# A three-pass attention and convolution kernel: first loads into buffers that are free early, strips and taps of the first image in turn, and a sum of k kept in another PSUM bank

## The chip, the cores and the metric

The kernel runs on one core of a Trainium2 chip (trn2). The metric is the device time of one execution in microseconds (us). Everything is float32. Engines are named as in the profile: PE is the tensor engine (PEld its weight loads), DVE the vector engine, ACT the scalar engine, POOL the GpSimd engine, SP the engine whose queue issues every DMA of this kernel. Each engine works through its own instructions in a fixed order and waits on semaphores for the others.

## What is computed

Eight images of 256 channels and 64 x 64 pixels go through two layers.

```
# layer 0: attention against keys and values of a 16 x 16 reduced image
xr  = layernorm_over_channels(conv4x4_stride4(x, w_sr)) * g + b
q   = w_q x ;  k, v = split(w_kv xr)               # 8 heads of 32
x   = x + gamma * w_out (softmax(q k^T / sqrt(32)) v)

# layer 1: linear attention on two scales
qkv = w_qkv x                                       # 3 * 256 channels
agg = w_pw (depthwise5x5(qkv))                      # 8 x 8 per group
for both (qkv, agg), in heads of 8 channels:
    kv  = sum over pixels of relu(k) (v, 1)^T       # 8 x 9; the last column is the sum of k
    att = (relu(q) kv)[:8] / ((relu(q) kv)[8] + 1e-15)
out = x + batchnorm(w_proj concat(att))
```

## The kernel before, in words

The work is three functions, called one after the other, with results handed on through DRAM. All loops are unrolled in Python. The code gives each tile a pool, a tag and a number of buffers; a tile framework then places pools in SBUF, one behind the other in the order in which a pass opens them, and derives every semaphore. A pass's pools lie over those of the pass before it, so a tile's first write waits until whatever tile lay there has been used for the last time. The framework also sets the order on each engine: an instruction that is ready in its own estimate may be put ahead of one that stands earlier in the code but isn't ready. In the trace, for example, the stores of zeros `border` (L624, called once an image) all stand on SP in the first stretch, and the copy L1129 stands some 7 us ahead of L1130, which follows it in the code.

**First pass** (`first_pass`, L575). `load_x(0)` issues the eight strips of image 0 (L599, 512 KB each), then seven constants are loaded (L589). `keys_values(0)` (L653) goes through 16 taps of the 4 x 4 convolution: each loads a weight tile `wsr` (256 KB, L662, four buffers) and does matmuls at L665. Tap f reads columns 256 f to 256 f + 255 of the image, so strip s (512 columns) holds what taps 2s and 2s + 1 read. Mean, variance, scale, k and v follow (L679 to L728). Then a loop over image, strip, channel half and key half does scores (L752), exponentials (L758), values (L769), denominators (L785), output (L803) and, six steps behind, qkv (L828). The next image's `keys_values` and the second pass's convolution weights (`conv_weights`, L632) are fed in between. Images alternate between two buffers of 32 KB a partition. qkv goes to DRAM as `planes`, keys as `kd`, values as `vd`.

**Second pass** (`second_pass`, L946). 64 units (two channel halves t, four groups k, eight images b; b innermost). A unit loads a convolution weight `w` (1.5 MB, once per eight units and kind, L963), cells `d` (578 KB, L969, one for keys and values and one for queries), tokens `kq` (512 KB, L976) and `vq` (four DMAs of 384 KB, L986). DVE makes differences of neighbouring cells, `c` (L996, L997, in `paired`); PE convolves them (L1054 and L1058, three banks `cv`). In `summed_raw` PE forms kv of the unconvolved keys (L1079) in a single bank, `raw`. In `summed` it does the same for the convolved ones (L1096). The sums of k are matmuls with a vector of ones. The bank `few` holds three results of a unit in turn: the k sum of the raw part, in column 0 (L1127, `ended_raw`), the k sum of the convolved part, in column 128 (L1135, `ended`), and the spread kv (L1142, `spread`). `ended_raw` copies kv out of `raw` (L1129) and the k sum out of `few` (L1130) into `mraw`, which is stored (L1131). `applied` (L1166) forms numerator and denominator in the bank pair `ng`, DVE divides (L1169, L1171) and transposes (L1178), and the result `att` is stored (L1180). The loop over u works on four units at once: the raw sum and first convolution of u, the sums of u - 1, the query convolution of u - 2, `applied` of u - 3. In the code, `summed_raw(u)` stands at the head of step u, and `ended_raw(u - 1)` in its middle.

**Third pass** (`third_pass`, L1230). 64 steps (image, half, class). `load_sums` (L1245) reads the kv sums of an image in eight DMAs (L1250) and spreads them over a mask; `loads` reads `raw` (L1275), `xs` (L1284) and `agg` (L1295). `flat` makes relu(q) (L1308), `applied` (L1343) the numerator, PE turns it (L1361), and `proj` (L1379) projects; ACT scales (L1388), DVE adds (L1397), and the result is stored (L1404). The code calls `loads(0)` ahead of its constants, and `loads(n + 2)` at each step n.

Of the kernel before, what the change touches and what calls it, by code (L numbers as in the profile page):

```python
# [574 lines left out]
def first_pass(ctx: ExitStack, tc: tile.TileContext, a, fine, planes, x2d, kd, vd, wtd):  # L575
# [4 lines left out]
    xpool = ctx.enter_context(tc.tile_pool(name="xpool", bufs=2))  # L580
# [6 lines left out]
    def load(src, name):  # L587
        t = const.tile(list(src.shape), F32, tag=name, name=name)
        nc.sync.dma_start(t, src)  # L589
        return t  # L590

    x_tiles = {}

    def load_x(b):
        x_tiles[b] = xpool.tile([P, 2, HW], F32, tag="x", name=f"x_{b}")
        src = a.xp[b].rearrange("(c p) n -> p c n", p=P)
        for s in range(NG):
            cols = slice(s * QB, (s + 1) * QB)
            nc.sync.dma_start(x_tiles[b][:, :, cols], src[:, :, cols])  # L599

    load_x(0)
    vec = load(a.vecs, "vec")
    wkv = load(a.w_kv, "wkv")
    wq = load(a.w_q, "wq")
    gam = load(a.gamma_s, "gam")
    wout = load(a.w_out, "wout")
    wqkv = load(a.w_qkv, "wqkv")
    wsmall = load(a.w_small, "wsmall")
# [11 lines left out]
    nil = const.tile([NB2 + 2, 8 * P], F32, tag="nil", name="nil")  # L620
# [11 lines left out]
    def conv_weights():  # L632
        for j in (2, 3, 0, 1):
# [4 lines left out]
            for i in range(8):  # L638
# [5 lines left out]
                    wsmall[:, j, gs].unsqueeze(2).to_broadcast([P, 2, 6 * 16, D1]),  # L644
# [8 lines left out]
    def keys_values(b):  # L653
# [51 lines left out]
        for ci in range(2):  # L705
            nc.vector.tensor_mul(xr[:, ci], xr[:, ci], rs)
            nc.vector.tensor_scalar(
                xr[:, ci], xr[:, ci], vec[:, 0, ci : ci + 1], vec[:, 1, ci : ci + 1], ALU.mult, ALU.add
            )
# [4 lines left out]
        for oc in range(2):  # L714
            ps = bank(f"k_{b}_{oc}")[:, :NK]
            for ci in range(2):
                nc.tensor.matmul(
                    ps, wkv[:, ci, oc * P : (oc + 1) * P], xr[:, ci], start=(ci == 0), stop=(ci == 1)
                )
            nc.scalar.copy(kk[:, oc], ps)  # L720
        yield
        for kc in range(2):
            ps = bank(f"v_{b}_{kc}")[:, :C]
            for ci in range(2):
                nc.tensor.matmul(
                    ps, xr[:, ci, kc * P : (kc + 1) * P], wkv[:, ci, C:], start=(ci == 0), stop=(ci == 1)
# [7 lines left out]
    def queries(b, s, c):  # L734
        ps = bank(f"q_{b}_{s}_{c}")
        for ci in range(2):
            nc.tensor.matmul(  # L737
                ps,
                wq[:, ci, c * P : (c + 1) * P],
# [59 lines left out]
    def added(b, s, att, oc):  # L799
        xt, cols = x_tiles[b], slice(s * QB, (s + 1) * QB)  # L800
        ps = bank(f"o_{b}_{s}_{oc}")
        for c in range(2):
            nc.tensor.matmul(ps, wout[:, c, oc * P : (oc + 1) * P], att[c], start=(c == 0), stop=(c == 1))  # L803
        nc.vector.scalar_tensor_tensor(  # L804
            xt[:, oc, cols], ps, gam[:, 0:1], xt[:, oc, cols], ALU.mult, ALU.add
# [19 lines left out]
    def qkv(b, s, st, j):  # L825
        ps = bank(f"qkv_{b}_{s}_{j}")
        for ci in range(2):
            nc.tensor.matmul(  # L828
                ps,
                wqkv[:, ci, j * P : (j + 1) * P],  # L830
# [35 lines left out]
    for _ in keys_values(0):  # L866
# [3 lines left out]
    q, es, att, fill = {0: queries(0, 0, 0)}, {}, {}, []  # L870
# [75 lines left out]
def second_pass(ctx: ExitStack, tc: tile.TileContext, a, planes, kd, vd, wtd, kvd, attd):  # L946
    nc = tc.nc
    B = a.x.shape[0]
    const = ctx.enter_context(tc.tile_pool(name="const2", bufs=1))
    two = ctx.enter_context(tc.tile_pool(name="two2", bufs=2))  # L950
# [7 lines left out]
    wt, data, cells, kqs, vqs = {}, {}, {}, {}, {}  # L958

    def load_weights(u, what):  # L960
        t, k, b = units[u]
        w = two.tile([P, 4, 6 * P], F32, tag=f"w{what}", name=f"w{what}_{t}_{k}")
# [3 lines left out]
    def load_cells(u, what):  # L966
        t, k, b = units[u]
        d = two.tile([P, 4, (NB + 1) ** 2], F32, tag=f"d{what}", name=f"d{what}_{u}", bufs=2)
        nc.sync.dma_start(d, planes[b, 2 * what + t][4 * k : 4 * k + 4].rearrange("g p e -> p g e"))  # L969
        data[u, what] = d.rearrange("p g (y x) -> p g y x", x=NB + 1)  # L970


    def load_tokens(u):
        t, k, b = units[u]
        kq = two.tile([P, 2, 4, P], F32, tag="kq", name=f"kq_{u}")
# [5 lines left out]
        vq = two.tile([P, 4, 6 * P], F32, tag="vq", name=f"vq_{u}", bufs=3)  # L981
# [9 lines left out]
    def paired(u, what):  # L991
        d = data[u, what]
        c = two.tile([P, 2 + what, 4, (NB + 1) * NB // 2], F32, tag=f"c{what}", name=f"c{what}_{u}")
# [28 lines left out]
    eps = const.tile([P, 1], F32, tag="eps", name="eps")  # L1022
# [19 lines left out]
    def convolve(u, what, i):  # L1042
        t, k, b = units[u]
        c, w, d = cells[u, what], wt[t, k, what], data[u, what]
# [77 lines left out]

    def ended_raw(u):
        t, k, b = units[u]
        few[u] = bank("few", f"few_{u}")
        col, ps = few[u][:, :1], raws.pop(u)
# [4 lines left out]
        nc.sync.dma_start(kvd[b, t][k], m)  # L1131

    def ended(u):
        col, m = few[u][:, 128:129], state[u, "m"]
# [5 lines left out]
    def spread(u):  # L1140
        ps = few.pop(u)[:, 256 : 256 + D0 + 4]
# [88 lines left out]
def third_pass(ctx: ExitStack, tc: tile.TileContext, a, planes, x2d, kvd, attd, out):  # L1230
    nc = tc.nc
    B = a.x.shape[0]
    const = ctx.enter_context(tc.tile_pool(name="const3", bufs=1))
    two = ctx.enter_context(tc.tile_pool(name="two3", bufs=2))
# [10 lines left out]
    def load_sums(b):  # L1245

        kvp = two.tile([P, 2, 4, D0 + 1], F32, tag="kvp", name=f"kvp_{b}")
        for t in range(2):
            for k in range(4):
                nc.sync.dma_start(  # L1250
                    kvp[k * D0 : (k + 1) * D0, t], kvd[b, t][k].rearrange("(f d) n -> d f n", f=4)
                )
        nc.vector.tensor_add(kvp[:, :, :2], kvp[:, :, :2], kvp[:, :, 2:])
        kva = two.tile([P, 2, D0 + 1], F32, tag="kva", name=f"kva_{b}")
        nc.vector.tensor_add(kva, kvp[:, :, 0], kvp[:, :, 1])

        m = two.tile([P, 2, P + NH], F32, tag="kvm", name=f"kvm_{b}")
# [10 lines left out]
    def loads(n):  # L1268
# [3 lines left out]
        raw = two.tile([P, 2, 4, 8 * (NB + 1)], F32, tag="raw", name=f"raw_{n}", bufs=3)  # L1272
# [9 lines left out]
        xs = two.tile([P, 2, 4, P], F32, tag="xs", name=f"xs_{n}", bufs=4)  # L1282
# [8 lines left out]
        if cls == 0:  # L1291

            g = two.tile([P, 2, 2, 1024], F32, tag="agg", name=f"agg_{n}")
# [43 lines left out]
    def applied(n, i):  # L1337
# [9 lines left out]
        tok = two.tile([P, 4, P], F32, tag="tok", name=f"tok_{n}_{i}", bufs=3)  # L1347
# [8 lines left out]
    def turned(n, i, tok):  # L1356
        if i == 0:
            atts[n] = two.tile([P, 2, 4, P], F32, tag="att", name=f"att_{n}")
# [8 lines left out]
    def proj(n, oc):  # L1367
# [18 lines left out]
        z = two.tile([P, 4, P], F32, tag="z", name=f"z_{n}_{oc}")  # L1386
# [181 lines left out]
```

## Time and profile before

| what | value |
|---|---|
| median of 10 runs | 4097.92 us (4095.25 to 4105.59) |
| profiled execution | 4094.31 us; its span 4092.5 us |
| PE busy | 3948.2 us, 96% of the span |
| DVE, ACT, POOL busy | 49%, 41%, 29% |
| moved by DMA | 691.32 MB, mean 169 GB/s |
| first matmul | at 20.95 us |
| last matmul of the first pass, first of the second | ends near 2147.4, starts at 2171.06 us |
| last matmul of the second pass, first of the third | ends near 3418.1, starts at 3437.64 us |

Times in the trace count from the start of the span. In a row of the timeline stand start, length, engine, line, operation, output and inputs by the program's tile names, sizes, and a count; in square brackets how long the engine had been idle before it and what ended that. A matmul of float32 operands appears as two PE records. Ends of matmuls are modelled.

### The profile page before, as it was taken

The page shows a single profiled execution, that of the slowest core. Times are in us where ns is not written, and L with a number is a line of the kernel's source. Part 1 is how long each engine was busy: PE and PEld are TensorE (multiplying, and loading weights), DVE is VectorE, ACT ScalarE, POOL GpSimd, SP SyncE. Part 2 cuts the span into 40 slices and gives each one's busy share as a digit, 9 for nine tenths or more (in the row PEclk, how much of TensorE's full clock was granted, in tenths as well). Part 3 has the DMA queues.
Part 4 walks back from the last instruction along what each step waited for, and adds up shares of the span by engine and source line. Part 5 has one row for each costly group of instructions (what it writes and reads, how often), then busy time and mean ns, then how long its engine had stood idle before and what let it go on. Part 6 is the DMA issues. An engine that isn't in the chain of part 4 may idle for free. (4 is left out here: it accounts for less than half of the span.)

```text
span 4092.5 us, 69474 instructions
## 1 busy us (share of the span) xinstructions
PE 3948.2 (96%) x27266; PEld 2344.5 (57%) x27266; DVE 2007.9 (49%) x2724; ACT 1659.9 (41%) x3505; POOL 1206.9 (29%) x1234
## 2 busy tenths in 40 slices
PE   7999999999999999999996999999999997999999
PEld 4343433434334344343335898898898895555655
DVE  2555343343444434434443676666676774444443
ACT  1445455454554544545541222222222223445544
POOL 1333233232332333333333343443444440000000
PEclk9999999999999999999998999999999998999999
DMA  7655435334443344433349787777777766877674
GB/s 239 180 173 154 132 98 147 102 103 143 105 136 110 101 143 106 132 107 93 95 111 272 227 229 228 207 224 225 213 222 226 211 179 153 227 208 226 203 228 139
DMA packets 582944, 691.32 MB, mean 169 GB/s; under 512 B 62928, under 2 KB 432080, under 8 KB 576336
## 3 DMA queue, kind: packets, MB, share of 16 engines
q1 hardware_dynamic: 582608, 686.79, 59.0%
q8 instruction: 216, 3.54, 0.4%
q14 instruction: 120, 0.98, 0.1%
HBM read 412.54 MB, written 274.10 MB: 168 GB/s over the span
## 5 line engine op out<-in xcount | busy, mean ns | idle before, releaser
L780 POOL TENSOR_TENSOR e<-e,e 128x512 f32<-128x512 f32 x512 | 651.2, 1304 | 1212.4 <-PE av L769 1206.8
L793 DVE RECIPROCAL rden<-den 128x512 f32<-128x512 f32 x128 | 429.7, 3357 | 699.1 <-PE den L785 699.1
L828 PE MATMUL qkv<-x,wqkv 128*128 128x512 f32 x1536 | 701.1, 600 | 0.3 <-DVE x L804 0.3
L758 ACT ACTIVATE e<-sc 128x512 f32<-128x512 f32 x1024 | 529.1, 603 | 415.8 <-PE sc L752 415.8
L828 PEld LDWEIGHTS qkv<-x,wqkv 128*128 128x128 f32 x1536 | 285.6, 191 | 372.7 <-issue 352.3
L1054 PE MATMUL cv<-w,c 128*128 128x128 f32 x3072 | 386.7, 280 | 23.6 <-DMA vq<-v 23.6
L1054 PEld LDWEIGHTS cv<-w,c 128*128 128x128 f32 x3072 | 360.4, 193 | 53.2 <-issue 26.0
L847 DVE STREAM_TRANSPOSE turned<-qkv 128x512 f32<-128x512 f32 x256 | 177.1, 707 | 329.0 <-ACT stage L837 288.9
L752 PE MATMUL sc<-q,kk 32*128 32x512 f32 x2048 | 323.4, 640 | 9.1 <-DVE turned L847 5.0
L1397 DVE TENSOR_TENSOR y<-z,xs 128x256 f32<-128x256 f32 x256 | 142.7, 642 | 315.4 <-ACT z L1388 307.9
L769 PE MATMUL av<-e,vv 128*32 128x512 f32 x2048 | 274.9, 609 | 0.0
L837 ACT COPY stage<-qkv 128x512 f32<-128x512 f32 x256 | 149.9, 585 | 300.0 <-PE qkv L828 300.0
L1070 ACT ACTIVATE r<-s 128x512 f32<-128x512 f32 x256 | 155.6, 628 | 279.1 <-DVE s L1069 272.9
L1096 PE MATMUL sums<-vq,r 128*32 128x288 f32 x4096 | 263.3, 408 | 0.0
L1388 ACT ACTIVATE z<-p,bn 128x256 f32<-128x256 f32 x256 | 133.5, 576 | 312.0 <-PE p L1379 235.7
L665 PE MATMUL sr<-x,wsr 128*128 128x256 f32 x1024 | 237.3, 387 | 21.5 <-DMA wsr<-in_w_sr_dram 21.5
L737 PE MATMUL q<-x,wq 128*128 128x512 f32 x512 | 254.3, 619 | 0.0
L1058 PE MATMUL cv<-c,w 128*128 128x128 f32 x2048 | 253.9, 278 | 0.0
L1379 PE MATMUL p<-att,wproj 128*128 128x512 f32 x512 | 248.7, 608 | 3.9 <-ACT att L1362 3.9
L1379 PE MATMUL p<-agg,wproj 128*128 128x512 f32 x512 | 241.1, 593 | 0.0
L665 PEld LDWEIGHTS sr<-x,wsr 128*128 128x128 f32 x1024 | 194.9, 193 | 80.0 <-issue 33.1
L1058 PEld LDWEIGHTS cv<-c,w 128*128 128x128 f32 x2048 | 240.7, 193 | 0.0
(121 smaller groups left out, 5093.9 us busy)
## 6 DMA issues: line engine op xcount, KB each, us to landing
vq<-v SPq DMA_DIRECT2D x256, 384.0 KB
planes<-stage SPq DMA_DIRECT2D x256, 289.0 KB
d<-planes SPq DMA_DIRECT2D x128, 578.0 KB
raw<-planes SPq DMA_DIRECT2D x128, 272.0 KB
x<-in_xp_dram SPq DMA_DIRECT2D x64, 512.0 KB
wsr<-in_w_sr_dram SPq DMA_DIRECT2D x128, 256.0 KB
x<-x SPq DMA_DIRECT2D x128, 256.0 KB
k<-turned SPq DMA_DIRECT2D x256, 128.0 KB
```

Of the source, the lines that this page charges most:

```text
L665: nc.tensor.matmul(ps[:, oc], w[:, ci, oc * P : (oc + 1) * P], xt[:, ci, f * NK : (f + 1) * NK], start=(f == ci == oc == 0), stop=(f == R ...
L737: nc.tensor.matmul(ps, wq[:, ci, c * P : (c + 1) * P], x_tiles[b][:, ci, s * QB : (s + 1) * QB], start=(ci == 0), stop=(ci == 1),)
L752: nc.tensor.matmul(scs[h], kks[b][rows, c, kc * P : (kc + 1) * P], qs[rows], start=True, stop=True)
L758: nc.scalar.activation(e, scs[h], AF.Exp, scale=D0**-0.5)
L769: nc.tensor.matmul(sums["av"][cols], vvs[b][:, kc, c * P + h * D0 : c * P + (h + 1) * D0], es[h], start=(kc == 0), stop=(kc == 1),)
L780: nc.gpsimd.tensor_tensor(es0[h], es0[h], es1[h], ALU.add)
L793: nc.vector.reciprocal(r, den)
L828: nc.tensor.matmul(ps, wqkv[:, ci, j * P : (j + 1) * P], x_tiles[b][:, ci, s * QB : (s + 1) * QB], start=(ci == 0), stop=(ci == 1),)
L1054: nc.tensor.matmul(out, x, m, start=(da == 0), stop=(da == 1))
L1058: nc.tensor.matmul(out, m, x, start=(da == 0), stop=(da == 1))
L1096: nc.tensor.matmul(ps[h * D0 : (h + 1) * D0, : 36 * D1].rearrange("p (r n e) -> p r n e", r=3, e=D1), kt[:, par, h, 2 * r + c], vq[:, r : ...
L1379: nc.tensor.matmul(ps.rearrange("p (f q n) -> p f q n", f=4, q=4), wproj[:, j, oc * P : (oc + 1) * P], src, start=(j == 0), stop=(j == 3),)
```

## The change

It has four parts. (1) Image 0's strips and taps are issued in turn, strip 0, taps 0 and 1, strip 1, and so on; the constants are loaded behind them, with `wq` first; the first `queries` call comes two steps of `keys_values` earlier. (2) The two image buffers, and the zeros `nil`, get pools of their own. The second pass opens its pools in another order: constants, then a pool `late2` (query differences `c0`, `eps`), then three data pools; the loads of unit 0 (`w1`, `d1`, `kq`, `vq`, with index 0) are in the first of them, those with index 1 in the second, and the query weights and cells in the third; the rest follows in `two2`. (3) The third pass does likewise: constants, `late3` (`tok`, `att`, `z`), then `data3` with all loads and sums, then the rest; the kv sums are stored so that one DMA for each t, two an image, reads them. (4) `ended_raw` puts its k sum into column 64 of the bank `raw`; `few` is taken in `ended` and holds two results.

```
-    xpool = ctx.enter_context(tc.tile_pool(name="xpool", bufs=2))
+    nilpool = ctx.enter_context(tc.tile_pool(name="nilpool", bufs=1))
+    xpools = [ctx.enter_context(tc.tile_pool(name=f"xpool{i}", bufs=1)) for i in range(2)]
...
-    load_x(0)
-    vec = load(a.vecs, "vec")
-    wkv = load(a.w_kv, "wkv")
...
+    def load_strip(b, s):
         src = a.xp[b].rearrange("(c p) n -> p c n", p=P)
+        cols = slice(s * QB, (s + 1) * QB)
+        nc.sync.dma_start(x_tiles[b][:, :, cols], src[:, :, cols])
+
+    def load_consts():
+        for n, src in (
+            ("wq", a.w_q), ("wkv", a.w_kv), ("vec", a.vecs), ("gam", a.gamma_s), ("wout", a.w_out),
+            ("wqkv", a.w_qkv), ("wsmall", a.w_small),
+        ):
+            load(src, n)
...
-    for _ in keys_values(0):
+    x_tiles[0] = xpools[0].tile([P, 2, HW], F32, tag="x", name="x_0")
+    ahead = keys_values(0)
+    for s in range(NG):
+        load_strip(0, s)
+        next(ahead)
+        next(ahead)
+    load_consts()
+    next(ahead)
+    first = queries(0, 0, 0)
+    for _ in ahead:
         pass
...
+    late = ctx.enter_context(tc.tile_pool(name="late2", bufs=2))
+
+    data = [ctx.enter_context(tc.tile_pool(name=f"data2_{i}", bufs=1)) for i in range(3)]
     two = ctx.enter_context(tc.tile_pool(name="two2", bufs=2))
...
-        w = two.tile([P, 4, 6 * P], F32, tag=f"w{what}", name=f"w{what}_{t}_{k}")
+        pool = data[k % 2 if what else 2]
+        w = pool.tile([P, 4, 6 * P], F32, tag=f"w{what}_{k % 2}", name=f"w{what}_{t}_{k}")
...
-        kq = two.tile([P, 2, 4, P], F32, tag="kq", name=f"kq_{u}")
+        kq = data[u % 2].tile([P, 2, 4, P], F32, tag=f"kq_{u % 2}", name=f"kq_{u}")
...
-        vq = two.tile([P, 4, 6 * P], F32, tag="vq", name=f"vq_{u}", bufs=3)
+        vq = data[min(u % 3, 1)].tile([P, 4, 6 * P], F32, tag=f"vq_{u % 3}", name=f"vq_{u}")
...
     def ended_raw(u):
         t, k, b = units[u]
-        few[u] = bank("few", f"few_{u}")
-        col, ps = few[u][:, :1], raws.pop(u)
+        ps = raws.pop(u)
+        col = ps[:, 64:65]
         nc.tensor.matmul(col, reds.pop((u, "raw")), ones, start=True, stop=True)
         m = two.tile([P, D0 + 1], F32, tag="mraw", name=f"mraw_{u}")
         nc.vector.tensor_copy(m[:, :D0], ps[:, :D0])
         nc.vector.tensor_copy(m[:, D0:], col)
-        nc.sync.dma_start(kvd[b, t][k], m)
+        nc.sync.dma_start(kvd[b, t][:, k], m)
 
     def ended(u):
-        col, m = few[u][:, 128:129], state[u, "m"]
+        few[u] = bank("few", f"few_{u}")
+        col, m = few[u][:, :1], state[u, "m"]
...
+    late = ctx.enter_context(tc.tile_pool(name="late3", bufs=2))
+    data = ctx.enter_context(tc.tile_pool(name="data3", bufs=2))
     two = ctx.enter_context(tc.tile_pool(name="two3", bufs=2))
...
         for t in range(2):
-            for k in range(4):
-                nc.sync.dma_start(
-                    kvp[k * D0 : (k + 1) * D0, t], kvd[b, t][k].rearrange("(f d) n -> d f n", f=4)
-                )
+            nc.sync.dma_start(kvp[:, t], kvd[b, t].rearrange("f k d n -> (k d) f n"))
```

## The prediction

> **What bounds the kernel now.** I read the busy times first, then the stages. The page gives TensorE (PE) 96% and nothing else above 57%:
>
> ```profile
> PE 3948.2 (96%) x27266; PEld 2344.5 (57%) x27266; DVE 2007.9 (49%) x2724; ACT 1659.9 (41%) x3505; POOL 1206.9 (29%) x1234
> ```
>
> So only PE's idle time can be saved: 4092.5 - 3948.2 = 144.3 us, plus the work done at a reduced clock beside it. The table by stage (columns: stretch; its length; busy time of PE, weight load, DVE, ACT, POOL; granted clock; DMA share; GB/s) says where it lies:
>
> ```profile
> 0.00:21.00 21.00, 0.05 (x1) 0.08 (x1) 0.21 (x3) 1.28 (x1) 2.41 (x11) 1.00 0.94 341
> ...
> 1000.00:2147.00 1147.00, 1147.00 (x4910) 466.41 (x4909) 469.60 (x401) 563.35 (x1176) 381.70 (x364) 1.00 0.42 112
> 2147.00:2171.00 24.00, 0.43 (x3) 0.19 (x1) 1.89 (x8) 0.58 (x1) 1.25 (x1) 0.60 0.93 278
> ...
> 3418.20:3437.70 19.50, 0.06 (x1) 0.07 (x1) 3.93 (x15) 1.20 (x4) 1.20 (x3) 0.50 0.46 114
> ```
>
> Inside a pass PE is full (1147 of 1147 us); it is empty for 21 us at the start, 23.6 between the first and second pass and 19.5 between the second and third. PE's own list of waits (who, for whom: us in total, times, longest) names the rest:
>
> ```profile
> PE few L1135 <- DVE mraw L1130: 40.3, 9, 8.0
> PE cv L1054 <- DMA vq<-v: 23.6, 1, 23.6
> PE sr L665 <- DMA wsr<-in_w_sr_dram: 21.5, 3, 21.0
> PE n L1343 <- DMA xs<-x: 19.5, 1, 19.5
> ```
>
> The three large single waits are first loads. The fourth, 40.3 us in nine stalls, lies in the second pass. The timeline around one of them:
>
> ```profile
> 2484.02 0.72 DVE L996 TENSOR_TENSOR c<-d 128x544 f32<-128x544 f32 x1 [7.70 <-DMA d<-planes]
> 2484.56 0.28 PE L1127 MATMUL few<-ones,red_raw 128*128 128x1 f32 x2
> ...
> 2489.86 0.14 DVE L1130 COPY mraw<-few 128x1 f32<-128x1 f32 x1
> ...
> 2490.15 0.56 PE L1135 MATMUL few<-ones,red_agg 128*128 128x1 f32 x2 [3.42 <-DVE mraw L1130]
> 2490.57 3.76 PE L1058 MATMUL cv<-d,w 128*128 128x128 f32 x16
> ```
>
> The d of the next unit lands late, DVE stands 7.70 us at L996, its queued work (among it the copy L1130) slips, and PE waits for that copy. In most units L1130 starts 1.14 us after L1127 ends, L1135 0.6 us later, and PE waits for nothing.
>
> **What the skill says.** The Trainium skill, "TensorE: Matmul & The Clock Gate", What's actually happening: an idle window of about 3.4 us drops the array to half clock, and busy time restores it. The trace agrees: granted clock 0.50 from 3420 to 3440, and 16 matmuls at L1058 take 3.76 us behind the stall, about 2.1 elsewhere. "PSUM — Partial Sum Buffer", PSUM bank collisions raise a hardware error: engines are to be kept apart by bank, not by address. The trace shows that guard: L1135 writes column 128 of few while L1130 reads column 0, and waits 40.3 us for it. "DMA: Bandwidth & Descriptors", Anatomy of one DMA: DMA engines don't wait; the issuing sequencer does, before dispatch. The trace agrees: SP stands among five att stores from 3401.42 to 3418.05, and the third pass's first load is issued at 3418.61.
>
> **The change, part by part,** against the profiled execution: span 4092.5, 4094.31 us outside. The median shown, 4097.92, is 3.6 above that; I subtract the savings from the median.
>
> *Start.* Now SP issues eight strips, seven constants and then the first tap (14.59 us); PE starts at 20.95. Ahead of that matmul lie 4.2 MB of strips, 2.2 MB of constants and 0.26 MB of taps. Afterwards strip 0 and tap 0 (0.8 MB) suffice. The stretch 10 to 20 us moved 396 GB/s and 0 to 10 us 285, so transfers begin at about 2.8 us and 0.8 MB take 2: PE starts near 5, at best 16 us earlier. The 128 matmuls at L665 take 30.8 us (104 in 25.05). Through tap 15, 8.4 MB must land: 25 us at the 341 GB/s of the first 21 us; constants make it 10.6 MB, 32 us; image 1's strips, which are issued in SP's gaps, 14.8 MB, 44 us. A tap waits for one of four buffers and then stands behind whatever has been issued. PE would end the taps at 36 with no such delay, at about 46 with all of it, against 52.3 now. I take 40: **gain 12** (6 to 16). The query matmuls moved ahead are the same four. The seven constants (5.25 to 14.59, 9.3 us of SP) are moved behind the taps in the code and fill SP's gaps; wq, vec and wkv are first used behind the taps, and wsmall, the last, only delays DVE's products at L641, one of which (1.76 us) now stands in the normalisation chain ahead of L681: a few us either way, within the range.
>
> *First to second pass.* Unit 0's w, d, kq and vq (4.2 MB) move to the pool laid over x_0's buffer, last used by image 6, hence free about one image, (2147 - 70) / 8 = 260 us, before the end. Their DRAM sources are long written. The cover: that stretch uses 0.42 of DMA, and SP has gaps; without it, the stores queued behind them would slip by the 0.34 + 0.43 + 0.77 + 4.33 = 5.9 us that w, d, kq and four vq take to issue now, and PE by less. Unit 1's loads lie over x_7 and stay behind 2147; SP then still issues stores until 2156.0, and d, taps, mix, three small constants, kq and vq by the rows now take about 14 us of issue, so unit 1's tokens land near 2173. PE meanwhile does unit 0 and the convolution of unit 1. One unit's work here is 3 x 1.92 (cv) + 0.75 (raw) + 4.05 (sums) + 0.5 = 11.1 us, two 22. Now they end at 2202.47. Then: 2147.4 + 22 + about 8 of waiting = 2177, 25 earlier; I take **gain 22** (14 to 27), since the order of SP's queue is not shown. What is late next: vq of unit 1.
>
> *Second to third pass.* Step 0's kvp, raw, xs and agg (3.2 MB, with wproj 3.8 MB; 11 us at 340 GB/s) lie over unit 62's and 63's buffers, free at about 3398, and no longer over att, stored at 3420.7. Fewer kvp issues (2 for 8 per image; 14 of them take 6.45 us ahead of raw now) remove that delay. Landing near 3412 to 3418, against PE's last matmul at 3418.1. Now PE has done two steps' first half at 3450.20: 32 us later, of which 7.5 is work at full clock, so 24.6 is lost. Left: some 3 us of chain (n, den, tok, at, att) and 3 of data. **Gain 18** (8 to 24). The bound below: att stores still ahead of them on SP.
>
> *The k sum in raw's bank.* The wait at L1135 loses its cause. But raw's bank is single. Now L1129 copies raw early (some 7 us before L1130) and frees it for the next unit's L1079. Afterwards the bank is held until both copies behind the k-sum matmul are done, and those stand in DVE's queue where L1130 stands now. L1079 of the next unit comes at the head of a unit's work and must move behind them. So the nine stalls stay and change their name to **raw L1079 <- DVE mraw**; what PE did ahead of the stall, raw (0.75 us), now follows it: 9 x 0.7 = 6. In the other units the copies end 1.14 + 0.33 = 1.5 us behind the k sum, while PE has cv(1) (1.9 us at L1054) to do: nothing, if L1079 is put behind that. Queued behind a waiting L1079: the unit's own cv and sums. Bounds: +27 where L1079 isn't moved (below), -40 at 0.6 us in each of 63 units. I take **-5**.
>
> *Nothing:* images in two pools of one buffer instead of one of two (same alternation, b mod 2); consts in a dictionary; the store layout of kv (128 rows of 132 bytes either way, 64 stores); c, eps, tok, att and z in pools of their own (same buffer counts); cells and weights over the same number of buffers. The steady loops keep their sizes; their cover is PE's own 96%.
>
> Sum: 12 + 22 + 18 - 5 = 47: 4097.9 - 47 = **4051**, own range 4030 to 4072.
>
> **Rivals.**
> *The k-sum stall really goes* (0.16). If the k sum runs early, in PE's gaps, raw is free in time. For: its inputs are ready a unit earlier. Against: PE has no gaps there, and L1127 stands at its place in the code now. Then in a stall PE runs L1135 and 16 cv (2.4 us), waits at L1166 for tok, then at the next cv for c; in the stall shown, that cv began at 2496.04 and its c is ready between 2491.6 and 2493.3. So 2.7 to 4.4 us a stall, about 3.2: 7 x 3.2 + 3.2 + 1.1 = 27, instead of -5: **4019**.
> *The loads don't come early* (0.16). SP is in order; behind waiting stores, first loads slip. For: five att stores over 16.6 us, stores until 2156. Then half of both boundaries stays (20 us) and the taps stand behind image 1 (5): **4076**.
> *Every unit waits for raw's bank* (0.10), the slower side. Place: L1079. If it is put right behind the k sum, it finds the two copies 1.5 us away, and cv(1) can't cover. 63 x 1.5 = 95 against a gain of 52: **4141**; it decides from 52 / 63 = 0.83 us per unit. For: the copies are behind s of the same unit in DVE's queue. Against: where a matmul's place depends on DVE now (L1166, placed two matmuls into the next cv at 3401.4), tok had been ready 0.7 us, so placing looks cautious.
>
> **How the numbers follow.** Main 0.55 at 4051; rivals 0.16, 0.16, 0.10; 0.03 left for a reshuffled order, on either side. Range 4014 to 4084: it holds the main case, nearly all of the first rival, most of the second. 0.2% is 8.2 us, about what a measurement of this kernel can tell from no change. Faster (below 4089.7): 0.55 + 0.16 + 0.15 = 0.86; within: 0.05; slower: 0.09.
>
> **What would show it.** First matmul near 5 us and L665 done by 40; PE's gap at the end of the first pass (near 2135) below 3 us, w, d and kq of unit 0 issued before it; the gap before L1343 below 6. No wait at L1135; about 40 us at L1079 for mraw L1130, in nine stalls. I am wrong if L1079 shows no wait, or one in most units, or if a boundary gap stays above 10.

## The result and the profile after

The changed kernel takes 4076.85 us (median of 9 runs, 4073.06 to 4086.64); the kernel before takes 4098.85 (median of 31 runs, 4090.13 to 4105.59). The ratio is 0.9949, 95% interval 0.9941 to 0.9957: 22 us saved, against a forecast of 47. Of all executions reported here one counts as slow and is left out of its ratio, one of f_raw_mid's at 8064.32 us. The profiled execution has a span of 4072.4 us, 20.1 less than before. Lines of `second_pass` are now 15 or 16 higher: the cv matmuls L1054 are L1070, raw L1079 is L1095, the k sum of the convolved part L1135 is L1151, and the copy L1130 is L1145.

The page's busy line and the table by stage of the changed kernel (columns as before: stretch; length; busy time of PE, weight load, DVE, ACT, POOL; clock; DMA share; GB/s):

```profile
PE 3960.9 (97%) x27266; PEld 2327.0 (57%) x27266; DVE 1926.1 (47%) x2724; ACT 1659.5 (41%) x3505; POOL 1199.8 (29%) x1234
...
0.00:5.53 5.53, 0.00 (x1) 0.03 (x1) 0.21 (x3) 1.28 (x1) 2.40 (x11) 1.00 0.66 196
2134.20:2147.80 13.60, 1.09 (x68) 0.89 (x66) 1.96 (x8) 0.58 (x1) 1.22 (x2) 0.62 0.87 213
```

PE starts at 5.5 us instead of 21. Its wait ahead of the second pass went from 23.6 us to about 12.5, and the one directly ahead of the third from 19.5 to 1.9. Ahead of the latter, still in the second pass, PE now waits 4.41 and 2.74 us, where it waited 2.05 before. Over the whole span PE is idle for 111.5 us instead of 144.3, which is 32.8 less, and yet the span is only 20 shorter. The first sign of why is in the first line: PE is busy for 12.7 us more than before (3960.9 for 3948.2), with the same 27266 instructions. Its list of waits (us in total, times, longest):

```profile
PE raw L1095 <- DVE mraw L1145: 45.9, 10, 8.0
PE cv L1070 <- POOL c L1016: 13.1, 2, 12.0
...
PE ng L1182 <- ACT r L1086: 4.4, 1, 4.4
...
PE ng L1182 <- DVE tok L1187: 2.7, 1, 2.7
PE n L1358 <- DVE tok L1187: 1.9, 1, 1.9
```

The k sum's stall has changed its name, from `few` to `raw`, and kept its size (40.3 in nine, now 45.9 in ten). One of the stalls after the change, from the timelines of DVE and PE:

```profile
2461.85 0.72 DVE L1012 TENSOR_TENSOR c<-d 128x544 f32<-128x544 f32 x1 [7.43 <-DMA d<-planes]
...
2468.43 0.14 DVE L1145 COPY mraw<-raw 128x1 f32<-128x1 f32 x1
...
2468.63 1.09 PE L1095 MATMUL raw<-vq,kq 128*32 128x32 f32 x64 [4.38 <-DVE mraw L1145]
```

It is the same chain as before: d late, DVE standing, the copy slipping, PE waiting. What differs lies in the units that do not stall. PE's timeline of a quiet unit, first before and then after:

```profile
2756.90 0.28 PE L1127 MATMUL few<-ones,red_raw 128*128 128x1 f32 x2
2757.04 2.03 PE L1054 MATMUL cv<-w,c 128*128 128x128 f32 x16
2758.91 0.28 PE L1135 MATMUL few<-ones,red_agg 128*128 128x1 f32 x2
```

```profile
2755.01 0.28 PE L1142 MATMUL raw<-ones,red_raw 128*128 128x1 f32 x2
2755.15 1.81 PE L1070 MATMUL cv<-w,c 128*128 128x128 f32 x14
2756.89 0.76 PE L1095 MATMUL raw<-vq,kq 128*32 128x32 f32 x64
2757.58 0.49 PE L1070 MATMUL cv<-w,c 128*128 128x128 f32 x2
2757.91 0.28 PE L1151 MATMUL few<-ones,red_agg 128*128 128x1 f32 x2
```

Before, raw (64 records of 128x32) stood directly ahead of `sums`, which has the same stationary shape, 128*32, and took 0.55 us from start to start. Now it lies inside the cv's 128*128 matmuls. From L1142 to L1151 pass 2.90 us, against 2.01 between the same places before: 0.89 more for work worth 0.55. No wait is shown in it. The unit's period, from the first `sums` matmul to that of the next unit, has a median of 18.31 us before and 18.63 after.

Put together, the lead over the kernel before along the span (last matmul of the first pass, the copy of the k sum in the third unit of the second pass, last cv, end) is 13.0, 28.8, 9.0 and 20.1 us. In the middle, 20 us of lead are lost.

### The profile page after: what moved, and what is told of

It is laid out like the page before. It is cut to its first block, busy times and chain, and to the rows that moved or that the text cites. A ratio compares the mean times of both kernels' runs of the same rounds, so it can differ in the third digit from the quotient of the medians.

```text
span 4072.4 us, 69470 instructions
## 1 busy us (share of the span) xinstructions
PE 3960.9 (97%) x27266; PEld 2327.0 (57%) x27266; DVE 1926.1 (47%) x2724; ACT 1659.5 (41%) x3505; POOL 1199.8 (29%) x1234
## 5 line engine op out<-in xcount | busy, mean ns | idle before, releaser
L1070 PE MATMUL cv<-w,c 128*128 128x128 f32 x3072 | 403.6, 282 | 13.1 <-POOL c L1016 13.1
L1070 PEld LDWEIGHTS cv<-w,c 128*128 128x128 f32 x3072 | 365.8, 193 | 45.2 <-issue 26.0
L1085 DVE TENSOR_TENSOR s<-cv,both 128x512 f32<-128x512 f32 x256 | 172.2, 672 | 140.0 <-PE cv L1070 95.2
```

The source lines that it names most:

```text
L1070: nc.tensor.matmul(out, x, m, start=(da == 0), stop=(da == 1))
```

## The experiments

No kernel below leaves out any of the work. "Period" is the median time from unit to unit in the second pass. "Excess" is the sum, over units longer than 19.5 us, of what they take above that median: it holds PE's waits in the stalls and also the matmuls at a lowered clock behind them, which is why it is 60 before where the waits alone are 40. "Tail" is the time from the end of the last cv matmul to the end of the span. These three come from the one profiled execution of each kernel, and separate executions differ by some us.

| kernel | median us | ratio to before, 95% interval | period | excess | tail |
|---|---|---|---|---|---|
| before | 4098.85 | | 18.31 | 60.0 | 678.7 |
| after | 4076.85 | 0.9949 (0.9941 to 0.9957) | 18.63 | 62.8 | 667.6 |
| c_start | 4083.93 | 0.9968 (0.9957 to 0.9979) | 18.32 | 60.9 | 677.9 |
| d_pools2 | 4078.90 | 0.9949 (0.9935 to 0.9962) | 18.31 | 70.1 | 670.4 |
| e_pools3 | 4104.35 | 1.0013 (1.0005 to 1.0022) | 18.31 | 70.2 | 679.9 |
| b_ksum | 4113.24 | 1.0040 (1.0027 to 1.0053) | 18.64 | 60.6 | 678.7 |
| m_no3 | 4061.86 | 0.9913 (0.9897 to 0.9928) | 18.31 | 63.0 | 671.8 |
| a_few | 4061.20 | 0.9915 (0.9901 to 0.9930) | 18.31 | 64.0 | 667.0 |
| f_raw_mid | 4185.54 | 1.0217 (1.0204 to 1.0230) | 19.11 | 114.1 | 678.6 |
| g_sums | 4034.50 | 0.9839 (0.9824 to 0.9854) | 18.31 | 35.6 | 669.8 |
| n_shape | 4041.04 | 0.9864 (0.9849 to 0.9879) | 18.68 | 22.0 | 667.8 |
| h_msk | 4064.69 | 0.9917 (0.9904 to 0.9931) | 18.31 | 67.5 | 665.9 |
| i_c1 | 4072.59 | 0.9930 (0.9916 to 0.9944) | 18.31 | 75.7 | 668.8 |
| q_sums_w4 | 4011.96 | 0.9787 (0.9774 to 0.9801) | 18.31 | 15.7 | 669.5 |

### One part undone, and each part alone

**a_few**: the changed kernel with the fourth part undone.

```
-        ps = raws.pop(u)
-        col = ps[:, 64:65]
+        few[u] = bank("few", f"few_{u}")
+        col, ps = few[u][:, :1], raws.pop(u)
...
-        few[u] = bank("few", f"few_{u}")
-        col, m = few[u][:, :1], state[u, "m"]
+        col, m = few[u][:, 128:129], state[u, "m"]
```

> The changed kernel with its fourth part undone: the sum of k goes back into the bank of the few sums (columns 0, 128 and 256). Theory A: the sum's own bank costs time in every unit of the second pass, because the 128x32 sum of k now runs between 128x128 matmuls of the second convolution and the tile shape has to change twice more; the trace has 18.63 us per steady unit against 18.31, so some 55 units give 0.32 us each, about 18 us. This kernel then takes about 4058 us (18 to 20 less than the changed kernel's 4077). Theory B (the prediction's): the fourth part costs nothing in the units and its stalls only change their names, and the missing gain went elsewhere, so this kernel takes about 4077 (within 4 us of the changed one), or up to 5 us more.

Measured: 4061.2 us, 15.6 below the changed kernel (A gave 18 to 20); the period is 18.31 again, the excess 64.0 for 62.8. Theory A holds in its mechanism and B falls: the fourth part costs about 16 us, and not through its stalls. (What lies between the 128*128 matmuls is raw's products, as the timelines above show; the k sum itself is 128*128.)

**b_ksum**: the same edit the other way round, on the kernel before.

> The kernel before with the fourth part alone: only the sum of k of raw moves into raw's bank. Theory A (two more changes of tile shape per unit): about 18 to 20 us slower, 4117 us, and the steady units at 18.6 us instead of 18.3. Theory B (the stalls change their names and no more): within 4 us of the kernel before. A third reading, that the wait on raw's bank is what costs: slower too, but then the trace must show the loss as waits at raw ahead of DVE's product with mask, of more than the 58 us that the few sums show now.

Measured: 4113.24, a ratio of 1.0040 (1.0027 to 1.0053), which is 16 us of loss; period 18.64. Its waits in the second pass at raw are 42.3 us in eight stalls, where `few` had 40.3 in nine, so the third reading, which needs more than 58, falls too. Both directions agree: 0.32 us in each of some 55 quiet units is 18, and the stalls stay as they are.

**c_start**: the kernel before with the first part alone.

```
-    for _ in keys_values(0):
...
+    ahead = keys_values(0)
+    for s in range(NG):
+        load_strip(0, s)
+        next(ahead)
+        next(ahead)
+    load_consts()
...
```

> The kernel before with the first part alone: strips and taps of the first image take turns in the load queue. Theory A: the first scores end 19 us earlier, some 5.5 of it is lost again within the first 365 us of the first pass where PE comes to wait for DVE, so about 13 us faster. The prediction's own figure was 12 (6 to 16). Rival: all of it is given back by the end of the first pass, as the later images' loads set its pace: within 4 us of the kernel before.

Measured: 0.9968 (0.9957 to 0.9979), 13 us. In its trace the first scores are 20.5 us earlier, the end of the first pass 16.5, the span 14.5.

**d_pools2**: the separate pools for x and the zeros, and the second pass's pools, alone.

```
+    data = [ctx.enter_context(tc.tile_pool(name=f"data2_{i}", bufs=1)) for i in range(3)]
...
-        d = two.tile([P, 4, (NB + 1) ** 2], F32, tag=f"d{what}", name=f"d{what}_{u}", bufs=2)
+        pool = data[u % 2 if what else 2]
+        d = pool.tile([P, 4, (NB + 1) ** 2], F32, tag=f"d{what}_{u % 2}", name=f"d{what}_{u}")
```

> The kernel before with the separate pools for the two buffers of x and for the zero edge, and the second pass's first loads in pools that are free early; nothing else. Theory A: the gap of PE between first and second pass shrinks by about 12 us (23.6 to 12: what comes last is then the buffer of c, laid over the first pass's pool, which comes free as a whole) and the sums of the first unit end some 16 us earlier, and the units hold that: about 16 us faster. The prediction's figure was 22 (14 to 27). Rival: the units of the second pass are paced by their loads and DVE and give it back: within 4 us of before.

Measured: 0.9949 (0.9935 to 0.9962), 21 us (16 to 27), where 16 were expected. The tail says where the rest is: it is 8 us shorter (670.4 for 678.7), although the third pass's code is as before. Its first load of raw is issued 10.8 us after the last cv matmul ends, 18.7 before, and PE's wait ahead of the third pass is 12.0 us instead of 19.5. With the second pass's buffers laid out otherwise, those of the third come free sooner, it seems; no more can be read here.

**e_pools3**: the third pass's pools and the layout of kv, alone.

```
+    data = ctx.enter_context(tc.tile_pool(name="data3", bufs=2))
...
-        raw = two.tile([P, 2, 4, 8 * (NB + 1)], F32, tag="raw", name=f"raw_{n}", bufs=3)
+        raw = data.tile([P, 2, 4, 8 * (NB + 1)], F32, tag="raw", name=f"raw_{n}", bufs=3)
```

> The kernel before with the third pass's buffers alone: its first loads go to pools that are free early, and the key-value tiles are laid out as in the changed kernel. Theory A: the gap ahead of the third pass closes, but the tail of the second pass is stretched, since DVE's product of mask with the key-value sums is ahead of the last units' work and waits 5 us for the mask's load, and PE behind it: 10 to 12 us faster. The prediction's figure was 18 (8 to 24). Rival: none of it stays, 0.

Measured: 1.0013 (1.0005 to 1.0022), 5 us slower. Both expectations miss. The tail is no shorter, 679.9 us for 678.7: with the second pass's pools as they were, the third pass's first load of raw is issued 16.0 us after the last cv matmul ends (18.7 before; in the changed kernel it is 14.9 ahead of that end). The loss is in the second pass, whose excess is 70.2 instead of 60.0. Why the stalls are longer there is open.

**m_no3**: the first and second part, without the third and fourth. The edit is that of c_start and d_pools2 together.

> The kernel before with the first and second part alone: neither the third pass's buffers nor the sum of k's bank. Theory after the first runs: the third part is worth 2 to 3 us on top of the second (with it PE's gap ahead of the third pass goes, but its early loads share the queues with the last att stores, DVE stands for those and for the mask, and the first projection starts no earlier), so 4063 us, 1 to 5 more than the kernel with only the fourth part undone (4061). The prediction's term: 18 us for the third part, so 4079.

Measured: 4061.86, against 4061.20 with the third part in it. By the ratios m_no3 saves 36 us, about the 13 and 21 of its two parts alone. The third part, for which 18 us had been forecast, adds nothing that the medians show, and each of them has an interval of 6 us to either side; in the traces the tail is 671.8 without it and 667.0 with it. It may be worth some 5 us or nothing; the runs don't settle it. PE's waits about this boundary, without the third part (m_no3) and with it (a_few):

```profile
PE n L1359 <- ACT q L1324: 11.9, 1, 11.9
PE ng L1182 <- DVE tok L1187: 2.9, 1, 2.9
PE p L1395 <- ACT att L1378: 2.7, 2, 2.0
PE at L1377 <- DVE tok L1364: 1.2, 2, 0.7
```

```profile
PE ng L1181 <- ACT r L1086: 4.1, 1, 4.1
PE p L1393 <- ACT att L1376: 2.9, 1, 2.9
PE ng L1181 <- DVE tok L1186: 2.7, 1, 2.7
PE n L1357 <- DVE tok L1186: 1.9, 1, 1.9
PE at L1375 <- DVE tok L1362: 1.8, 3, 1.1
```

The single wait of 11.9 us at n has shrunk to 1.9, but others have come up: the lists sum to 18.7 us without the third part and 13.4 with it; the first projection starts 23.6 us after the last cv matmul instead of 24.8. In the changed kernel one can read what lengthens the tail:

```profile
3397.18 0.74 SPq L1261 DMA_DIRECT2D msk<-in_mask_dram  x1
...
3406.24 0.29 DVE L1274 TENSOR_TENSOR kvm<-msk,kva 128x128 f32<-128x128 f32 x1 [5.26 <-DMA msk<-in_mask_dram]
...
3409.19 2.26 PE L1182 MATMUL ng<-bd,r 128*128 128x144 f32 x8 [4.41 <-ACT r L1086]
```

The mask for the third pass is issued behind 2.2 MB of other early loads (kvp, raw, xs and an agg) and lands 9 us later. DVE's product with it has been put ahead of the last units' work, so DVE stands 5.26 us, then ACT, then PE at `ng`.

**h_msk**: a_few with the mask and the vector loaded first.

```
-    msk = const.tile([P, P], F32, tag="msk", name="msk")
+    msk = data.tile([P, P], F32, tag="msk", name="msk", bufs=1)
     nc.sync.dma_start(msk, a.mask)
+    vec = data.tile([P, 6, 2], F32, tag="vec", name="vec", bufs=1)
+    nc.sync.dma_start(vec, a.vecs)
...
```

> The changed kernel with the fourth part undone, and the third pass's mask and vector loaded first among its loads, into a pool that is free early. Theory: DVE's wait of 5.3 us for the mask at the end of the second pass goes, and PE's waits behind it with it: about 5 us less than the kernel with only the fourth part undone. Rival: the wait goes and PE's next wait (for ACT's scaled sums) takes its place: within 2 us.

Measured: 4064.69, 3.5 above a_few, so the 5 us of the theory do not come; the figure is outside the rival's 2 us as well, but the two intervals overlap almost wholly (0.9904 to 0.9931, 0.9901 to 0.9930). The wait for the mask is gone from the trace, and the tail is 665.9 for 667.0. DVE then waits 2.97, 2.16 and 1.80 us for att stores to land so that it can write the next att, and ACT up to 3.90 us for raw. In the trace the rival's mechanism is seen, the next waits take its place, though other ones than it named. That the early loads hold up the second pass's last stores in the queues fits this, but was not tried apart.

### Is it the change of tile shape?

**f_raw_mid**: the kernel before with `summed_raw(u)` called behind `ended_raw(u - 1)`; no bank is changed.

```
         if now:
             positive(u)
-            summed_raw(u)
...
         if now:
+            summed_raw(u)
             convolve(u, 1, 1)
```

> The kernel before with one thing moved and no bank changed: the call that makes the raw keys' products is issued after the few sums of raw and ahead of the second convolution's second half, so that 128x32 matmuls lie among 128x128 ones as in the changed kernel, while the sum of k stays in the few bank. If the change of tile shape is what the fourth part costs: 0.3 us in each of about 62 units, 18 to 22 us slower than the kernel before. If the cost is in sharing raw's bank (its wait for DVE's mask product): within 5 us of the kernel before.

Measured: 4185.54, 88 us slower, four times the most that either theory gives, so the time decides nothing. The call moved more than PE's order. DVE's largest wait in its second pass, and PE's:

```profile
DVE den L1169 <- ACT den L1168: 498.8, 64, 15.1
```

```profile
PE ng L1166 <- ACT r L1070: 51.4, 21, 6.6
```

Before, DVE waits there for 103 us. So the framework seems to have put DVE's and ACT's instructions into another order, on which the units wait. But the trace has 23 units like this one, in which nothing waits between the two k sums:

```profile
2709.14 0.28 PE L1127 MATMUL few<-ones,red_raw 128*128 128x1 f32 x2
2709.35 0.76 PE L1079 MATMUL raw<-vq,kq 128*32 128x32 f32 x64
2710.05 2.05 PE L1054 MATMUL cv<-w,c 128*128 128x128 f32 x16
2711.93 0.28 PE L1135 MATMUL few<-ones,red_agg 128*128 128x1 f32 x2
```

From L1127 to L1135 pass 2.79 us, against 2.01 before: 0.78 more, again for raw's 0.55, with no bank changed. Of the 0.34 us that the fourth part costs in a quiet unit beyond raw's own time, 0.23 are found here with the banks as before.

**n_shape** adds one small matmul to g_sums (below), near the place where the changed kernel has raw. Its result is not read.

```
                     nc.tensor.matmul(out, x, m, start=(da == 0), stop=(da == 1))
+                    if i == 1 and g == 2 and da == 1 and u - 1 in sums:
+                        v = vqs[u][:, 1, 1, 0].rearrange("p h e -> p (h e)")
+                        nc.tensor.matmul(sums[u - 1][:D0, 352:384], v, v, start=True, stop=True)
```

> The changed kernel with the sum of k of the convolved part in a spare column of the sums bank (4034 us), plus one added matmul of 32x32 in each unit, put after 14 of 16 records of the second convolution, where the changed kernel has the raw keys' products. Its result goes to columns that nothing reads, and neither a bank nor a wait is changed for any other instruction. If the change of tile shape between 128x128 matmuls is what the fourth part costs: 0.2 to 0.35 us in each of 63 units, 13 to 22 us more. If the shape is free: under 2 us more (the matmul itself is about 0.02 us), and the fourth part's cost lies in its bank.

The edit puts the matmul after 12 of the 16 records, not 14. And one wait is changed, in the stalled units: the added matmul writes the bank `sums`, so it waits there for DVE's product p, 10.0 us in five stalls, where in g_sums the k sum of the convolved part waits 13.6 in six. In quiet units nothing waits at this bank. A quiet unit:

```profile
2737.10 0.28 PE L1146 MATMUL few<-ones,red_raw 128*128 128x1 f32 x2
2737.24 1.58 PE L1070 MATMUL cv<-w,c 128*128 128x128 f32 x12
2738.75 0.25 PE L1073 MATMUL sums<-vq 128*32 128x32 f32 x2
2738.93 0.71 PE L1070 MATMUL cv<-w,c 128*128 128x128 f32 x4
2739.48 0.28 PE L1154 MATMUL sums<-ones,red_agg 128*128 128x1 f32 x2
```

From L1146 to L1154 pass 2.38 us, against 2.01 without the small matmul: 0.37 for two records that take 0.02 where raw's 64 take 0.55. The period is 18.68 for 18.31 in g_sums, and within 0.1 us of that in most units. So one excursion into the other shape costs about 0.35 us here, 0.23 in f_raw_mid's place, without a wait in the quiet units and without the k sum in raw's bank. A small matmul of the *same* shape was not added as a control; the nearest thing in the trace is the k sum L1146, also two records, from whose start to the next cv pass 0.14 us (2737.10 to 2737.24). Some of the price may be that of any visit, then, but most of it is not. The median moves less than the expected 13 to 22 us: 4041.04 against 4034.50, 6.5 us (10 by the ratios). The reason stands in the table: 0.37 in some 55 quiet units is 20, but the excess fell by 13.6. A slower PE has less to wait for the same late load, which would explain it; that was not tried apart.

### What stands behind the stalls

**g_sums**: a_few with the k sum of the *convolved* part in a spare column of the bank `sums`. `few` is then not written between the raw k sum and the copy.

```
+        sums[u] = ps
...
-        col, m = few[u][:, 128:129], state[u, "m"]
+        col, m = sums.pop(u)[:, 320:321], state[u, "m"]
```

> The changed kernel with the sum of k of raw back in the few bank, and in its place the sum of k of the convolved part moved to a spare column of the bank of the sums, so that the few bank is not written again after the second convolution and PE doesn't wait there for DVE's product with mask. No tile shape is added between 128x128 matmuls. Theory: nine stalls of together about 40 us at the few sums shorten by the 2 to 3 us that PE can go on with work: 15 to 28 us less than the kernel with the fourth part undone. Rival: PE stands a few matmuls later at ng or at the next c, since the load of d that DVE waited for is late whatever PE does: within 4 us of it.

Measured: 4034.5, 26.7 below a_few, in the expected range; the excess falls from 64.0 to 35.6. It is the gain that the prediction's first rival gave to the change itself (27 us), reached by moving the other k sum. What is left in the second pass:

```profile
PE sums L1151 <- DVE p L1123: 13.6, 6, 3.6
PE ng L1182 <- DVE tok L1187: 5.7, 4, 4.8
PE ng L1182 <- ACT r L1086: 2.2, 1, 2.2
```

**q_sums_w4**: g_sums with the weight of the next group loaded in quarters.

```
-        if now and units[u][2] == 4 and u + 4 < n_all:
-            load_weights(u + 4, 1)
+        if now:
+            load_part(u, 1)
...
+        nc.sync.dma_start(wt[t, k, what][:, part], wtd[2 * what + t][:, 4 * k + part])
```

> The kernel with the sum of k of the convolved part in the sums bank (4034 us), and the 1.5 MB convolution weight of the next group loaded in four quarters, one unit each, instead of at once. Theory: the one large load ahead of the cells d is what makes d late in one unit of eight; the waits left in the second pass at the sums and at ng, 26 us in all in the trace, go down by half or more: 10 to 20 us less, 4014 to 4024. Rival: d is late for other loads as well, and four small delays replace a large one: within 5 us.

Measured: 4011.96 us, 22.5 below g_sums, more than the 10 to 20 expected, and a ratio of 0.9787 (0.9774 to 0.9801) to before: the fastest version here. The excess goes from 35.6 to 15.7, and all that is left of it lies in the first nine units. So the load of w is what made d late once in eight units.

But the quarters did not run one in each unit, as the code has them. SP's timeline around such a unit, first in g_sums and then in q_sums_w4:

```profile
2441.23 1.10 SPq L977 DMA_DIRECT2D w<-wt  x1
2446.38 0.53 SPq L1196 DMA_DIRECT2D att<-att  x1
2447.00 2.30 SPq L984 DMA_DIRECT2D d<-planes  x2
```

```profile
2436.93 1.04 SPq L988 DMA_DIRECT2D w<-wt  x1
2438.44 1.96 SPq L994 DMA_DIRECT2D d<-planes  x2
2442.01 0.53 SPq L1206 DMA_DIRECT2D att<-att  x1
2442.59 1.44 SPq L988 DMA_DIRECT2D w<-wt  x3
```

One quarter stands ahead of d and three together behind it. In g_sums, as before, d stands in these units behind w *and* behind an att store for which SP has to wait: it is issued 17.3 us into the unit (from its first `sums` matmul), in the other units and in q_sums_w4 at 13.1. DVE gets past its wait for d at 9.2 us of the next unit in g_sums and at 2.6 in q_sums_w4; in this unit 4.2 of these 6.6 us are the earlier issue, and the other 2.4 the time from issue to use (10.2 and 7.8 us). So the larger part of the cure is d's place on SP, and the smaller the load ahead of d. To issue the whole w behind d was not tried.

### What holds the first boundary

In the changed kernel, w of unit 0 is issued at 1942.32 and its last vq at 1960.60, as forecast; raw of unit 0 runs at 2135.03. Then PE's and DVE's timelines:

```profile
2135.03 0.81 PE L1095 MATMUL raw<-vq,kq 128*32 128x32 f32 x64 [0.56 <-ACT stage L838]
2147.79 7.66 PE L1070 MATMUL cv<-w,c 128*128 128x128 f32 x52 [11.95 <-POOL c L1016]
```

```profile
2146.47 0.72 DVE L1012 TENSOR_TENSOR c<-d 128x544 f32<-128x544 f32 x1 [11.13 <-DMA planes<-stage]
```

DVE does not write c before the first pass's last store (`planes`) is done: c's buffer lies in `two2`, the pool that by its order covers the first pass's large pool. By the description of the kernel before, a tile waits for whatever tile lay in its place. Here it seems to wait for the whole pool: in i_c1 below another tile of `two2` waits for the same store. The addresses are not in the trace, so this is a likely reading and not shown.

**i_c1**: a_few with c's two buffers in pools that are free early. The edit also moves the small tiles p, kv and mixed into `late2` and c0 out of it.

```
-        pool = two if what else late
-        c = pool.tile([P, 2 + what, 4, (NB + 1) * NB // 2], F32, tag=f"c{what}", name=f"c{what}_{u}")
+        pool, tag, bufs = ((late, data[1])[u % 2], f"c1_{u % 2}", 1) if what else (two, "c0", 2)
+        c = pool.tile([P, 2 + what, 4, (NB + 1) * NB // 2], F32, tag=tag, name=f"c{what}_{u}", bufs=bufs)
...
-        p = two.tile([P, 36, D1], F32, tag="p", name=f"p_{u}", bufs=1)
+        p = late.tile([P, 36, D1], F32, tag="p", name=f"p_{u}", bufs=1)
...
```

> The changed kernel with the fourth part undone, and the two buffers of the cell differences c of the first convolution moved out of the pool that lies over the first pass's large pool, into pools that are free early. Theory: PE's gap between the first and second pass, 13.4 us now, shrinks to some 3 to 6, since c was waiting for a whole pool of the first pass to come free; then the tokens of unit 1 are late next, so 3 to 8 us less than the 4061 us of the kernel with only the fourth part undone. Rival: the gap is set by something else (the store or the load of the planes): no change within 2 us.

Measured: 4072.59, 11 us above a_few (6 by the ratios, and the intervals overlap); both expectations of the time fall. The wait for c is gone: cv starts 2.4 us after the last matmul of the first pass, with raw between. But the next tiles of the same pool are then the ones that wait, DVE's `mraw` first and `red_raw` after it:

```profile
2149.12 0.19 DVE L1144 COPY mraw<-raw 128x32 f32<-128x32 f32 x1 [9.52 <-DMA planes<-stage]
```

```profile
PE few L1150 <- DVE mraw L1145: 50.1, 10, 8.4
PE few L1142 <- DMA taps<-in_w_taps_dram: 7.0, 1, 7.0
PE few L1142 <- POOL red_raw L1048: 6.5, 1, 6.5
```

By the second unit's copy the kernel is 4.7 us behind a_few, 2.4 of which it had at the end of the first pass already. The rest of the loss is in the stalls (excess 75.7 for 64.0), and why they are longer is open, as in e_pools3.

## Why the prediction was wrong, step by step

The time lay within the range, but the sum was more than twice the gain. Against the trace (13, 16, 11 and -20 make the 20 of the span) its terms stand as follows. The 4076.85 us lie outside the main case's own range (4030 to 4072); that the wide range holds them is owed to a rival whose mechanism did not occur.

- **Start, 12 forecast, 13 measured: the mechanism is right, the size in part luck.** PE began at 5.53 ("near 5") and ended the taps at 37.5 ("40"), 14.8 us earlier, and the first scores came 19 us earlier, more than forecast. The lead then fell to 13.5 within some 380 us, where PE comes to wait for DVE, a loss that the prediction doesn't have. In the other kernels with this first part it is 10 to 16.5 us at the end of the first pass. (The sums for 10.6 and 14.8 MB give 31 and 43 us, not 32 and 44, which changes nothing.)
- **First to second pass, 22 forecast, about 16 at its place.** The step that failed is "about 8 of waiting" with "What is late next: vq of unit 1". The first loads did come early, and were not what came last: DVE could not write c for 11.13 us, until the first pass's last store was done, and the prediction has c's buffer nowhere in this sum ("same buffer counts"). The "gap ... below 3 us" did not come. Why c's place came free so late is argued above, not shown.
- **Second to third pass, 18 forecast, 11 measured, of which the third part itself has 0 to 5.** The step that failed is "Left: some 3 us of chain ... and 3 of data". n's wait went from 19.5 to 1.9 as forecast ("the gap before L1343 below 6"), but waits of 5.26 us on DVE and 4.41, 2.74 and 3.05 on PE came up. The other 7 or so came with the second pass's pools, by the tails of m_no3 (671.8 for 678.7) and d_pools2, where n waits 12 us instead of 19.5; the forecast gave that part nothing there. Which of its buffers does it was not tried. (A misreading beside it: eight kvp issues, 3.65 us, stand ahead of raw before, not 14 and 6.45.)
- **The k sum, -5 forecast, -16 measured (-20 at its place in the trace, with other losses in it).** "The nine stalls stay and change their name to raw L1079 <- DVE mraw" is right to the letter. The step that failed is the next: "In the other units ... nothing, if L1079 is put behind that". L1095 was put *inside* cv(1), two records before its end, and there each visit costs 0.32 us without a wait (18.63 for 18.31). The prediction priced waits and put at nothing that a moved group of matmuls can itself cost more among other neighbours: 0.32 x 55 = 18 us in each direction of the test, 16 by the medians. This is the largest miss of the sum.

The rivals: "the k-sum stall really goes" is refuted (45.9 us remain). "The loads don't come early", at 4076, has the right number for the wrong reason: they were issued at 1942 to 1960 and from 3388.89, well ahead. "Every unit waits for raw's bank" is refuted as a wait, but it was right that every unit pays, at 0.32 us instead of the 1.5 of its price and the 0.83 at which it would have decided.

What stays open: where in the first 380 us the start's 5.5 us are lost; why c's place came free so late; whether the third part is worth anything; and why the stalls' excess varies between 60 and 76 us among kernels that do not touch their cause. In all of these d is issued at the same place in the later stalled units (17.3 us, or 18.1 with the k sum in raw's bank), so that difference lies between d's issue and its landing.

## What to carry to other kernels

When an edit moves matmuls, look at the stationary shape of their new neighbours as well as at their waits, and compare the period of a quiet unit before and after: 0.3 us a unit shows in no list of waits. After closing a gap, ask which tile waits next: here one wait of 11.9 us mostly came back as smaller ones, and another moved to the next tile of its pool. A stall with a late load behind it is cured at the load: a cut of one 1.5 MB transfer, which let d go ahead of most of it, gave 22.5 us, as much as the whole change. Read in the trace where the pieces were issued; it need not be where the code has them.

## What the runs showed of the hardware that was not expected

- A visit of 128*32 matmuls among 128*128 ones costs about 0.35 us beyond the matmuls' own time, whether the visit has 2 records (0.37 in all) or 64 (0.89, of which 0.55 are their own); directly behind a k sum, in f_raw_mid, it cost 0.23. In n_shape the rows around it show it on both sides: the 12 cv records ahead take 1.51 us where 12/16 of 1.87 is 1.40, and the 4 behind take 0.55 for 0.47.
- A stall costs more than its wait. The nine waits before sum to 40.3 us and the stalled units take 60.0 us too long. The Trainium skill, "TensorE: Matmul & The Clock Gate", What's actually happening, states the lower clock after an idle window. The traces agree: in b_ksum, behind a wait of 5.55 us, 16 cv records at L1058 take 3.76 us, and 2.2 in a quiet unit; the granted clock is 0.51 from 2341.3 to 2347 us, right behind such a wait, and 1.00 from 2456 to 2462.
- One store that has to wait holds up the loads behind it on the same queue: in g_sums, with att ahead of d on SP, d is issued 17.3 us into the unit instead of 13.1.
